# The last softmax-sum addition of a unit as an accumulating DMA, in a Macaron block on one Trainium2 core

## The chip, the cores and the metric

The kernel runs on one core of a Trainium2 chip. The metric is the device time of one execution in microseconds (us), as the median of several runs. The engines are named as in the profile: PE is TensorE's matmul row and PEld its weight loads, DVE is VectorE, ACT is ScalarE, POOL is GpSimd, SP is SyncE. "L797" is line 797 of the kernel before the change.

## The reference

Four sequences of 1024 tokens with 128 features pass through three residual steps:

```
x = x + 0.5 * ffn(layernorm(x))
x = x + attention(layernorm(x))        # attention adds its own input too
x = x + 0.5 * ffn(layernorm(x))

ffn:        8 experts; weights from a sigmoid router
            out = sum over e of w[e] * (silu(x Wg[e]) * (x Wu[e])) Wd[e]
attention:  h = layernorm(x) * scale + bias
            c_q, c_kv = h w_down_q^T, h w_down_kv^T          # 64 wide each
            q, k, v   = up-projections of them, 16 heads of 64; rotary on q and k
            out       = softmax(q k^T / 8) v, heads joined, times w_out^T, plus input
```

Everything is float32. The part that matters here is the softmax: each query's 1024 exponentials have to be summed, and that sum (the denominator) divides the query's output.

## The kernel before

The kernel has three stages that overlap at their edges: the first feed-forward (to about 220 us), attention (about 220 to 1490 us), and the second feed-forward.

Attention is cut into 64 **units** U. A unit is one pair of heads of one sequence and one half (512) of its queries. A unit has eight **slots**, one for each block of 128 keys; slot `s = 8 * U + c`. For a slot and each of the two heads `hh`, `score` (L781) makes a 128 x 512 block of transposed scores on PE, in four matmuls, the last of which subtracts the row maximum, and ACT (L785) writes its exponential to a tile `p` of 128 keys x 2 heads x 512 queries. There are eight `p` buffers, so a slot takes the buffer of the slot eight before it. `values` (L804) multiplies each `p` block with the latent values on PE and adds up the eight slots of a unit in the bank `psc`. `passA` (L755, L756) makes scores of units that come 15 slots later, from which DVE takes the row maxima; the maxima of a unit go through DRAM (`d<-m`, then `maxr<-d`) to become a row.

The **denominators** are made in two steps. First the eight `p` blocks of a unit are added element by element into a tile `acc` of 128 x 1024 float32. `accumulate` (L797) does that on POOL: the first addition joins slots 0 and 1, and each later slot adds one more, seven in all. Then `den` (L816) sums `acc` over its 128 keys: matmuls with a matrix of ones, four for the two heads' halves, into a PSUM tile that ACT copies to `dsb` (L818). From there the sums go through DRAM (L822, L824) to a column layout `dT`, and `outp` (L839 to L854) divides by them.

`direct(U)` says how many of a unit's last `p` blocks are left out of POOL's additions and go to `den` by themselves, as four more matmuls each on PE. Before the change it is 1 for every third unit up to U = 53 (18 units), and 0 for the others.

The order on every engine is written out by hand. The main loop runs over **groups** g of four slots, two groups to a unit. In a group the program issues, in this order: the score matmuls of four slots with the `passA` matmuls between them; after every second group `den` of the unit that ended one group earlier (`self.den(g // 2 - 1)`); some steps of the rotary embedding and some loads; then the values of the four slots before. So the scores of unit U are in groups 2U and 2U + 1, and `den(U)` stands on PE behind the scores of group 2U + 2 and ahead of the values of the second half of unit U.

POOL's queue holds, besides the additions, one subtraction of 128 x 1024 per step of the rotary embedding (L680, `eo<-eo,hi_r`, one per unit as long as that work lasts), and small pieces of the router and the norms. All DMAs are issued from SP's queue: heads' loads (`QT<-qs`, `KT<-ks`), loads for the rotary embedding (`C_l<-cs`) and its stores (`qs<-eo`, `qs<-hi_r` and the same for `ks`), and the small transfers of maxima and denominators. SP's queue is in order, and it waits for `d<-m` to land before it issues `maxr<-d`.

In the last unit, `den(63)` stands on PE ahead of the last values and of the second feed-forward.

Of the kernel before, what the change touches and what calls it, by code (L numbers as in the profile page):

```python
# [13 lines left out]
ALU = mybir.AluOpType  # L14
# [4 lines left out]
B, S, D = 4, 1024, 128  # L19
# [21 lines left out]

def direct(U):

    return 1 if U % 3 == 2 and U < 56 else 0


class Kernel:
# [741 lines left out]
    def accumulate(self, s):  # L789

        nc = self.nc
        U, c = divmod(s, 8)
        if c == 0:
            self.acc_of[U] = self.accp.tile([128, 2, 512], F32, name="acc")
        elif c < 8 - direct(U):
            acc = self.acc_of[U]
            nc.gpsimd.tensor_tensor(acc, self.p_of[s - 1] if c == 1 else acc, self.p_of[s], ALU.add)  # L797
# [10 lines left out]
    def den(self, U):  # L808

        nc = self.nc  # L810
        osb = self.osb_of[U] = self.op2.tile([128, 512], F32, name="osb")
        pd = self.aux()
        parts = [self.p_of[8 * U + c] for c in range(8 - direct(U), 8)] + [self.acc_of[U]]
        for k, part in enumerate(parts):
            for n in range(4):
                nc.tensor.matmul(pd[32 * n:32 * n + 32, 0:256], self.ones, part[:, n // 2, 256 * (n % 2):256 * (n % 2) + 256], start=k == 0, stop=k == direct(U))  # L816
        dsb = self.op1.tile([128, 256], F32, name="dsb")
        nc.scalar.copy(dsb, pd[:, 0:256])  # L818
        dT = self.ms.tile([128, 8], F32, name="dT")

        d1 = self.dram.tile([4, 256], F32, name=f"d1_{U % 4}")
        nc.sync.dma_start(out=d1, in_=dsb[0:128:32, :])  # L822
        last = U == 2 * 8 * B - 1
        self.at(self.group + 1, lambda: nc.sync.dma_start(out=dT, in_=d1.rearrange("(h x) (y p) -> p (h x y)", x=2, p=128)), "mid")  # L824
        self.at(self.group + (4 if last else 3), lambda: self.outp(U, osb, dT), "side")
# [328 lines left out]
```

## Time and profile before

| what | value |
|---|---|
| median of 3 runs | 1651.11 us (1650.53 to 1651.83) |
| profiled execution, own time from first to last instruction (span) | 1648.4 us |
| PE busy | 1593.2 us, 97% |
| PEld busy | 1033.2 us, 63% |
| DVE busy | 1317.6 us, 80% |
| ACT busy | 1013.5 us, 61% |
| POOL busy | 1456.0 us, 88% |
| DMA, SP's queue | 210.28 MB, 50.6% of 16 engines |
| POOL additions L797 | 430 of 2.38 us |
| den's matmul instructions L816 | 512 from `acc`, 144 from `p` |
| granted PE clock, mean | 0.994 |

The profile is of one execution. Its span goes from the first to the last instruction; the profile has no other time of its own for that execution, so the median of the runs is compared with the span. A group line reads: line, engine, operation, output <- inputs, shapes, count, then busy us and mean ns of one, then the idle time of that engine just before these instructions and what ended it. A wait line reads: who waited <- for whom: us in total, times, longest. A timeline line reads: start us, duration us, engine, line, operation, count, and in brackets the idle time before it. A float32 matmul appears as two instructions, so four matmuls of `den` are eight rows; their ends are modelled, so rows of PE overlap and the distance between starts is the better measure. Instructions that issue a DMA are not counted as busy.

### The profile page before, as it was taken

What the parts mean: (1) busy time and instruction counts of PE and PEld (TensorE: products, weight loads), DVE (VectorE), ACT (ScalarE), POOL (GpSimd) and SP (SyncE); (2) the same over time, 40 slices, a digit from 0 to 9 for tenths busy, and PEclk for the clock granted to TensorE, in tenths of its full rate; (3) what the DMA queues carried; (4) which work ended last, traced back from release to release, by engine and by line L of the source; (5) the groups of instructions that cost most, each with busy time, mean ns of one, the idle gap of its engine ahead of it and who ended that gap; (6) DMA issues with size and microseconds to landing.
All of it is one profiled execution on the core that took longest, in us unless ns stands there. A gap on an engine that the chain in (4) does not pass through costs nothing.

```text
span 1648.4 us, 31237 instructions
## 1 busy us (share of the span) xinstructions
PE 1593.2 (97%) x11044; PEld 1033.2 (63%) x11044; DVE 1317.6 (80%) x2417; ACT 1013.5 (61%) x2220; POOL 1456.0 (88%) x833
## 2 busy tenths in 40 slices
PE   7998989999999999999999999999999999998998
PEld 5876765566566665666565666666566655656776
DVE  6556668888988888888899889889988868616897
ACT  4675666666666666666666656666566655654555
POOL 5668889999999989999999999999999999895676
PEclk9999999999999999999999999999999999999999
DMA  7025557555555655555555556666655532114443
GB/s 226 1 65 166 155 141 168 142 142 130 134 140 140 142 142 134 146 140 138 131 138 142 129 143 152 150 147 141 141 140 149 130 66 53 36 57 138 140 133 103
DMA packets 241149, 212.28 MB, mean 129 GB/s; under 512 B 157664, under 2 KB 170592, under 8 KB 240224
## 3 DMA queue, kind: packets, MB, share of 16 engines
q1 hardware_dynamic: 240992, 210.28, 50.6%
q8 instruction: 87, 1.43, 0.4%
q14 instruction: 70, 0.57, 0.1%
HBM read 130.39 MB, written 79.82 MB: 128 GB/s over the span
## 4 chain that ended last, share of the span: by engine, by line
PE 68%; POOL 3%; DVE 3%; ACT 2%; issue 2%; POOLq 0%; DVEq 0%; ACTq 0%
PE psc L804 24%; PE ps_s L781 21%; PE ps_a L755 6%; PE psx L781 3%; PE ps_s L521 3%; PE ps_s L816 2%; PE psx L476 2%; PE psx L839 2%; POOL acc L797 2%; PE psx L647 2%; ACT p L785 1%; PE ps_s L839 1%; POOL p L529 1%; PE psc L521 1%; DVE m L756 1%
## 5 line engine op out<-in xcount | busy, mean ns | idle before, releaser
L797 POOL TENSOR_TENSOR acc<-acc,p 128x1024 f32<-128x1024 f32 x366 | 872.6, 2384 | 56.3 <-ACT p L785 30.8
L756 DVE TENSOR_REDUCE m<-ps_a 128x1 f32<-128x512 f32 x1024 | 684.8, 688 | 158.0 <-PE ps_a L755 136.2
L785 ACT ACTIVATE p<-ps_s 128x512 f32<-128x512 f32 x896 | 478.2, 602 | 230.7 <-PE ps_s L781 197.1
L781 PE MATMUL ps_s<-QT,KT 64*128 64x512 f32 x2688 | 548.3, 397 | 3.1 <-DVE eo L663 3.0
L804 PE MATMUL psc<-p,ckn 128*64 128x512 f32 x2048 | 468.8, 600 | 0.0
L781 PEld LDWEIGHTS ps_s<-QT,KT 64*128 64x128 f32 x2688 | 351.2, 185 | 138.8 <-issue 76.3
L755 PE MATMUL ps_a<-KT,QT 64*128 64x512 f32 x1024 | 417.9, 419 | 5.0 <-DVE m L756 3.5
L804 PEld LDWEIGHTS psc<-p,ckn 128*64 128x64 f32 x2048 | 135.8, 137 | 257.3 <-issue 252.3
L781 PE MATMUL ps_s<-maxr,one_row 64*128 64x512 f32 x896 | 237.0, 391 | 0.0
L755 PEld LDWEIGHTS ps_a<-KT,QT 64*128 64x128 f32 x1024 | 184.5, 184 | 36.4 <-DVE m L756 12.8
L797 POOL TENSOR_TENSOR acc<-p 128x1024 f32<-128x1024 f32 x64 | 152.4, 2381 | 14.2 <-ACT p L785 11.9
L806 ACT COPY osb<-psc 128x512 f32<-128x512 f32 x64 | 37.6, 587 | 193.3 <-PE psc L804 193.3
L680 POOL TENSOR_TENSOR eo<-eo,hi_r 128x1024 fp32r<-128x1024 f32 x55 | 132.0, 2400 | 0.0
L781 PEld LDWEIGHTS ps_s<-maxr,one_row 64*128 64x128 f32 x896 | 122.3, 185 | 13.5
L781 PE MATMUL psx<-QT,KT 64*128 64x512 f32 x384 | 110.2, 393 | 0.0
L529 POOL TENSOR_TENSOR p<-eo,p 128x512 fp32r<-128x512 f32 x42 | 62.7, 1499 | 40.6 <-ACT p L528 33.1
L425 POOL TENSOR_TENSOR X<-X,dtmp 128x512 f32<-128x512 f32 x54 | 69.1, 1280 | 32.1 <-ACT dtmp L424 31.0
L852 DVE SCALAR_TENSOR_TENSOR X<-ps_s,rT,X 128x128 f32<-128x128 f32 x248 | 68.8, 339 | 26.4 <-PE ps_s L839 26.4
L849 ACT ACTIVATE psx<-psx,rT 128x128 f32<-128x128 f32 x248 | 85.4, 344 | 6.0
L672 ACT CAST hi_r<-eo 128x512 fp32r<-128x512 f32 x128 | 72.9, 615 | 18.8 <-POOL eo L667 14.0
L785 ACT ACTIVATE p<-psx 128x512 f32<-128x512 f32 x128 | 76.9, 601 | 4.4 <-issue 2.1
L781 PEld LDWEIGHTS psx<-QT,KT 64*128 64x128 f32 x384 | 71.1, 185 | 8.5
(237 smaller groups left out, 2388.2 us busy)
## 6 DMA issues: line engine op xcount, KB each, us to landing
C_l<-cs SPq DMA_DIRECT2D x128, 256.0 KB
QT<-qs SPq DMA_DIRECT2D x256, 128.0 KB
KT<-ks SPq DMA_DIRECT2D x256, 128.0 KB
qs<-hi_r SPq DMA_DIRECT2D x32, 512.0 KB
qs<-eo SPq DMA_DIRECT2D x32, 512.0 KB
ks<-hi_r SPq DMA_DIRECT2D x32, 512.0 KB
ks<-eo SPq DMA_DIRECT2D x32, 512.0 KB
rt<-wt SPq DMA_DIRECT2D x52, 256.0 KB
```

Source lines behind the costliest of these rows:

```text
L425: nc.gpsimd.tensor_tensor(X[:, t:t + 4, :], X[:, t:t + 4, :], tmp, ALU.add)
L529: (nc.gpsimd if m < N - 1 else nc.vector).tensor_tensor(sh[:, 1, :], hp, self.f(sh[:, 0, :]), ALU.subtract)
L672: nc.scalar.copy(w["hi"][:, k, :], w["eo"][:, k, :])
L680: nc.gpsimd.tensor_tensor(w["eo"].bitcast(F32R), w["eo"], self.f(w["hi"]), ALU.subtract)
L755: nc.tensor.matmul(self.psA[hh], self.QT[P % 3][r, 0, q0:q0 + 128], self.KT[P % 3][r, 0, kk * 512:kk * 512 + 512], start=True, stop=True)
L756: nc.vector.tensor_reduce(m[0][:, hh, qb, kk:kk + 1], self.psA[hh], AX.X, ALU.max)
L781: nc.tensor.matmul(ps, w, x, start=k == 0, stop=k == 3)
L785: nc.scalar.activation(self.p_of[s][:, hh, :], ps, AF.Exp, scale=0.125)
L797: nc.gpsimd.tensor_tensor(acc, self.p_of[s - 1] if c == 1 else acc, self.p_of[s], ALU.add)
L804: nc.tensor.matmul(self.psC[64 * hh:64 * hh + 64, :], self.ckn[b % 2][:, c, :], self.p_of[s][:, hh, :], start=c == 0, stop=c == 7)
L849: nc.scalar.activation(po[0][:, c], po[0][:, c], AF.Identity, scale=rT[:, i:i + 1])
L852: nc.vector.scalar_tensor_tensor(x, po[1][:, i * 128:(i + 1) * 128], rT[:, 4 + i:5 + i], x, ALU.mult, ALU.add)
```

## The change

The seventh addition (slot 7) of every unit but the last is no longer an instruction of POOL's but a DMA, issued from POOL's queue, which adds the tile `p` of slot 7 to `acc` in place. `direct` is 0 for those units, so no `p` block goes to PE by itself. For the last unit (U = 63) `direct` is 3: POOL makes four additions (slots 0 to 4), and the blocks of slots 5, 6 and 7 go to `den` as twelve more matmuls. The last line of the diff only makes the end of `den`'s accumulation follow the number of blocks.

```diff
 def direct(U):
 
-    return 1 if U % 3 == 2 and U < 56 else 0
+    return 3 if U == 2 * 8 * B - 1 else 0
...
         if c == 0:
             self.acc_of[U] = self.accp.tile([128, 2, 512], F32, name="acc")
+        elif c == 7 and not direct(U):
+            nc.gpsimd.dma_start(out=self.acc_of[U], in_=self.p_of[s], accum_op=ALU.add)
         elif c < 8 - direct(U):
             acc = self.acc_of[U]
             nc.gpsimd.tensor_tensor(acc, self.p_of[s - 1] if c == 1 else acc, self.p_of[s], ALU.add)
...
         for k, part in enumerate(parts):
             for n in range(4):
-                nc.tensor.matmul(pd[32 * n:32 * n + 32, 0:256], self.ones, part[:, n // 2, 256 * (n % 2):256 * (n % 2) + 256], start=k == 0, stop=k == direct(U))
+                nc.tensor.matmul(pd[32 * n:32 * n + 32, 0:256], self.ones, part[:, n // 2, 256 * (n % 2):256 * (n % 2) + 256], start=k == 0, stop=k == len(parts) - 1)
```

The DMA reads `p` and `acc` and writes `acc`. It waits for the sixth addition and for the exponentials of slot 7; `den` waits for it, and so do the next user of that `p` buffer (slot 7 of the next unit) and of that `acc` buffer (two units later).

## The prediction

> **What bounds the kernel now.** The page's busy shares come first, then the costliest groups, then the waits. TensorE is busy for 97% of the span and GpSimd for 88%; the windows of 100 us from 250 to 1350 us show TensorE at 98 to 100 and GpSimd at 93 to 97.
>
> ```profile
> PE 1593.2 (97%) x11044; PEld 1033.2 (63%) x11044; DVE 1317.6 (80%) x2417; ACT 1013.5 (61%) x2220; POOL 1456.0 (88%) x833
> L797 POOL TENSOR_TENSOR acc<-acc,p 128x1024 f32<-128x1024 f32 x366 | 872.6, 2384 | 56.3 <-ACT p L785 30.8
> L797 POOL TENSOR_TENSOR acc<-p 128x1024 f32<-128x1024 f32 x64 | 152.4, 2381 | 14.2 <-ACT p L785 11.9
> ```
>
> GpSimd's 430 additions are 1025 us of its 1456. But being busy is not being waited for. The waits, longest first, have only these rows in which TensorE waits for an addition (the first is its weight load, which runs ahead):
>
> ```profile
> PEld ps_s L816 <- POOL acc L797: 6.8, 1, 6.8
> PE ps_s L816 <- POOL acc L797: 5.9, 1, 5.9
> ```
>
> One wait in 64 units, and the timeline places it in the last unit. GpSimd is nearly full, yet in the other 63 units it finishes in time. So what it is relieved of is worth little; what TensorE is relieved of, or made to wait for, counts. TensorE runs its program in order: a wait of den's matmuls holds up the values and scores queued behind them.
>
> **What is taken off.** GpSimd: 18 direct units have 6 additions and 46 have 7, 430 in all; afterwards 63 have 6 and the last has 4, 382 in all. 48 x 2.38 us = 114 us of GpSimd, off the path by the reading above: I count it at nothing. What hides it is TensorE's own work in each unit; ACT's waits on L797, 10.5 us in four places, are the most that it could return, and only the range has them.
>
> TensorE: den's group for a direct unit is this, in the timeline.
>
> ```profile
> 704.98 0.64 PE L816 MATMUL ps_s<-p,ones 128*32 128x256 f32 x8
> 705.44 0.61 PE L816 MATMUL ps_s<-acc,ones 128*32 128x256 f32 x8
> 705.99 3.65 PE L804 MATMUL psc<-p,ckn 128*64 128x512 f32 x16
> ```
>
> The p part delays the acc part by 0.46 us. From den to den, units 15 to 53 take 19.98 us after a direct den and 19.65 after another: of 0.45 us of TensorE, 0.33 reaches the time, a factor of 0.73 (the rest was VectorE's and ScalarE's to wait for anyway). 18 x 0.33 = 6.0 us gained; 8.1 if all counted.
>
> The last unit:
>
> ```profile
> 1477.64 3.65 PE L804 MATMUL psc<-p,ckn 128*64 128x512 f32 x16
> 1487.18 1.08 PE L816 MATMUL ps_s<-acc,ones 128*32 128x256 f32 x8 [5.89 <-POOL acc L797]
> ```
>
> Its additions on GpSimd start at 1468.85 and 1471.29 (two), then, after two L173 pieces, at 1477.49 (four to 1487.12). With four in all the last ends near 1479.9, before TensorE is free at 1481.29. So 5.9 us go, and three more blocks cost 3 x 0.45 = 1.3: 4.6 gained, and the feed-forward behind it starts that much earlier. Gains together: 6.0 + 4.6 = 10.6 us.
>
> **What is added.** 63 accumulating DMAs of 512 KB, each behind the sixth addition on GpSimd's queue, and den waits for their landing. Behind the DMA's issue stand L680's subtraction and the next unit's first addition, which had 2.4 us of the seventh addition in its place; an issue under 2.4 us delays nobody (SP's take 0.3 to 0.6). Behind den's wait on TensorE stand 16 values matmuls and the next group. The allowance can be read, here in unit 45:
>
> ```profile
> 1129.47 10.10 POOL L797 TENSOR_TENSOR acc<-acc,p 128x1024 f32<-128x1024 f32 x4 [0.74 <-ACT p L785]
> 1142.12 0.64 PE L816 MATMUL ps_s<-acc,ones 128*32 128x256 f32 x8
> ```
>
> These are additions 4 to 7. The sixth ends after three, at 1136.8, and den starts at 1142.1: 5.3 us. A lighter GpSimd does not bring that forward: the fourth addition had waited for ScalarE's exponentials (0.74), so the sixth ends three additions after those. The same reading in all 63 units has a median of 4.9 us, with 8 in 10 between 3.8 and 5.8.
>
> No row has an accumulating transfer, nor any on GpSimd's queue. The nearest are SP's:
>
> ```profile
> 1125.78 0.39 SPq L56 DMA_DIRECT2D qs<-eo  x1
> 1138.75 0.34 SPq L56 DMA_DIRECT2D d<-m  x1
> 1140.85 0.57 SPq L56 DMA_DIRECT2D maxr<-d  x1
> ```
>
> maxr<-d waits for d<-m, so 4 KB have landed 2.1 us after issue; on average it is 0.34 of issue and 158.1 / 64 = 2.47 of wait, 2.8. For the 512 KB of qs<-eo, the DMA view of 1126 to 1129 us shows its first bytes at 1126.7 and some 380 GB/s: one pass takes 1.4 us. An addition must read both operands, so I take two passes: 2.1 + 2.8 = 4.9 us in quiet, 2.8 + 2.8 = 5.6 on average. The DMA engines are 42 to 62% busy in four such allowances; I take 5.2. Bounds: one pass and a quiet fixed part, 3.5; at worst SP's longest wait and its issue, 4.8, with two passes at the 269 GB/s of 1137.3 to 1139.0, 3.9: 8.7.
>
> The excess over the allowance, unit by unit and summed over the 63: 4.6 us at a latency of 3.5, 13.6 at 4.5, 34.2 at 5.2, 115 at 6.6, 247 at 8.7. With the factor 0.73: 3.4, 9.9, 25.0, 84 and 180. At 5.2 the balance is 25.0 - 10.6 = +14.4 us; break-even is a latency of 4.55.
>
> The Trainium skill's page "DMA: Bandwidth & Descriptors", in "Anatomy of one DMA", gives a transfer of GpSimd's queue 2.0 us and bytes over 436 GB/s: as an estimate 3.2 us here, which would hide it and leave about -8 us. "Collectives: The Full Stack", under "The bandwidth ceiling", speaks against the change: an add in the DMA engines needs two source reads and halves the rate; both pages together give an estimate of 4.4 us, a balance of -2. No run here shows either; the sum above uses neither.
>
> The other load: the transfers add 63 x 2.8 = 176 us at full rate to a DMA share of 51% of the span, some 11 points. SP's loads of the next pair and of C_l are issued a group (9.7 us) or more ahead, so I cost the collisions at nothing beyond the latency; without that cover, one C_l late by 0.5 us in each of the 55 steps that L680 counts would cost 0.73 x 27 = 20 us.
>
> The profiled execution's span is 1648.4 us, 2.7 below the runs' median of 1651.11. 1648.4 + 14.4 = 1662.8, and with that offset 1665.5.
>
> **Rivals.** *The transfer is hidden* (latency under 4.3 us). For it: den comes a whole score phase after the exponentials, and one pass is only 1.4 us. Then 3 to 9 us of excess remain against 10.6: 1643 to 1648. With no excess, all 8.1 us of the direct blocks and 7 us of ACT's waits, 1648.4 - 8.1 - 4.6 - 7 + 2.7 = 1631. This ends on the faster side and decides from 4.3 us down. *The add is slow in the DMA engines* (8.7 us or more): every unit waits, 180 us: about 1821. Against it: the DMA share has room, and TensorE's clock and SP's rate show no strain. *GpSimd's issue costs as much as the addition that it replaces:* then GpSimd keeps 18 x 2.4 us more than before, with L680 and the next additions late by that; GpSimd's idle time before additions, 70 us in all, takes it, and the time stays near that of the forecast. *The change does nothing but move the tail*, if the queue's transfer lands exactly at den: 1651 - 4.6 = 1646.5, within the first rival.
>
> **How the numbers follow.** The measurement can tell 0.2%, 3.3 us. Waits of 0.2 to 2 us a unit (latency 4.7 to 7): 0.45, and this is the forecast. Slow add (above 7 us): 0.11. Hidden: 0.38. Balanced within 3.3 us (4.3 to 4.7): 0.06. So faster 0.38, same 0.06, slower 0.56. The forecast's own range is 1654 to 1743, the ends of that latency by the same sum. The range of 8 in 10 takes in most of the hidden case, from 1638 (no excess and 8.1 us of direct blocks), and ends at a latency of 6.6 us: 1648.4 + 84 - 10.6 + 2.7 = 1724.
>
> **What would show it.** Right: den's L816 is preceded on TensorE by idle time put down to a DMA, in most units, 0.5 us on average; 382 additions; GpSimd's share falls to near 82%; the last unit's 5.9 us gone. Wrong: no idle time at L816 and a spacing near 19.6 us (hidden), or 3 us and more in every unit (slow add). A GpSimd issue above 2.4 us, or SP's loads found late by TensorE, would break the two terms that I cost at nothing.

## The result and the profile after

The changed kernel runs at 1788.5 us (median of 4 runs, 1779.3 to 1791.5) against 1650.8 for the kernel before on the same chip: 1.0817 times as long, interval 1.0797 to 1.0838. The direction of the forecast came true; the size was 137.7 us where 14.4 were forecast. The profiled execution's span is 1787.1 us, 138.7 more than before, and the mean granted TensorE clock is 0.971 where it was 0.994.

The code has moved by two lines: the DMA is L796, the additions are L799, the values L806, den L818. From the page: busy shares, GpSimd's DMA queue, the chain that ended last by engine, three groups, and the DMA issues.

```profile
PE 1628.2 (91%) x10924; PEld 1041.5 (58%) x10924; DVE 1323.4 (74%) x2417; ACT 1014.5 (57%) x2220; POOL 1398.6 (78%) x848
...
q0 software_dynamic: 9072, 33.03, 9.5%
...
PE 32%; DMA 20%; POOL 16%; issue 7%; ACT 5%; DVE 1%; SPq 1%; POOLq 0%; DVEq 0%; ACTq 0%
...
L799 POOL TENSOR_TENSOR acc<-acc,p 128x1024 f32<-128x1024 f32 x318 | 754.2, 2372 | 220.7 <-ACT p L785 201.0
...
L806 PE MATMUL psc<-p,ckn 128*64 128x512 f32 x2048 | 502.6, 636 | 0.0
...
L818 PE MATMUL ps_s<-acc,ones 128*32 128x256 f32 x512 | 44.1, 415 | 108.5 <-DMA acc<-p 107.0
...
acc<-p POOLq DMA_DIRECT2D x63, 512.0 KB, 6.7
```

From the page of before, the chain and the values:

```profile
PE 68%; POOL 3%; DVE 3%; ACT 2%; issue 2%; POOLq 0%; DVEq 0%; ACTq 0%
...
L804 PE MATMUL psc<-p,ckn 128*64 128x512 f32 x2048 | 468.8, 600 | 0.0
```

GpSimd is relieved as computed (318 + 64 = 382 additions). Its busy time falls by 57.4 us only, not by 114: the 63 issues, 0.88 us each, are counted in it here, unlike SP's, and L680's subtractions have become slower. Before its additions it now stands idle for 220.7 us in place of 56.3, 201.0 of them for ScalarE's exponentials, where it was 30.8. Den waits 107.0 us for the DMA, where before it waited 5.9 us for an addition, once. The chain is the largest contrast: before it was 68% TensorE and 3% GpSimd; now it is 32% TensorE, 20% this DMA and 16% GpSimd. One transfer takes 6.7 us from issue to landing (4.5 to 9.1), where the prediction took 5.2 from the end of the sixth addition.

The values (L806) have the same number of instructions as before and 502.6 us of busy time where it was 468.8, 33.8 more. TensorE's rows of the timeline show where that comes from: two units in a row, the first of which did not have to wait.

```profile
1212.37 0.64 PE L818 MATMUL ps_s<-acc,ones 128*32 128x256 f32 x8
1212.94 3.65 PE L806 MATMUL psc<-p,ckn 128*64 128x512 f32 x16
1222.25 3.65 PE L806 MATMUL psc<-p,ckn 128*64 128x512 f32 x16
1234.54 0.64 PE L818 MATMUL ps_s<-acc,ones 128*32 128x256 f32 x8 [3.11 <-DMA acc<-p]
1235.11 5.35 PE L806 MATMUL psc<-p,ckn 128*64 128x512 f32 x16
```

After a stand of 3.11 us the same 16 instructions take 5.35 us in place of 3.65. The windows (span of the window, then busy us and counts of PE, PEld, DVE, ACT, POOL, then granted clock, DMA share, GB/s) say why:

```profile
1225.00:1231.00 6.00, 6.00 (x50) 4.34 (x48) 4.92 (x9) 3.56 (x7) 5.62 (x6) 1.00 1.02 215
1235.00:1238.30 3.30, 3.30 (x14) 1.03 (x12) 1.18 (x3) 0.37 (x1) 3.22 (x2) 0.58 0.06 0
```

The granted clock falls from 1.00 to 0.58 just behind the stand. So the two large entries are 107.0 - 5.9 = 101.1 us of waiting and 33.8 us of slower values, 134.9 of the 138.7.

Why the waits add up, and are not absorbed, stands in the chain of the same unit, from den to den, in order of time (start, length, what):

```profile
1212.44 0.57 PE ps_s L818 x8
1213.01 3.58 PE psc L806 x16
1216.60 1.12 PE ps_s L781 x5
...
1218.06 1.10 ACT p L785 x2
...
1219.22 0.95 POOL acc L799
1220.17 1.48 issue
...
1221.69 2.36 POOL acc L799
...
1224.13 2.38 POOL acc L799
...
1226.81 7.59 DMA acc<-p
1234.40 0.14 issue
1234.54 0.59 PE ps_s L818 x5
```

It is a closed loop. Den holds up the values behind it, these hold up the next scores, the scores hold up the exponentials, those the fourth addition, then follow the fifth, the sixth and the DMA, and the DMA holds up the next den. One turn is 1234.54 - 1212.44 = 22.1 us, and that has become the unit: from den to den, units 2 to 54 take 22.2 us on average (19.9 to 24.7) where they took 19.8 (19.0 to 21.0). As an estimate from these pieces: with an addition of 2.4 us where the transfer and its handovers take 8.0, the turn would be 16.5 us, and TensorE's own work would set the time, as it did before.

### The profile page after: what moved, and what is told of

Same layout as the page of the kernel before. It is cut to its first block, busy times and chain, and to the rows that moved or that the text cites. A ratio compares the mean times of both kernels' runs of the same rounds, so it can differ in the third digit from the quotient of the medians.

```text
span 1787.1 us, 31134 instructions
## 1 busy us (share of the span) xinstructions
PE 1628.2 (91%) x10924; PEld 1041.5 (58%) x10924; DVE 1323.4 (74%) x2417; ACT 1014.5 (57%) x2220; POOL 1398.6 (78%) x848
## 4 chain that ended last, share of the span: by engine, by line
PE 32%; DMA 20%; POOL 16%; issue 7%; ACT 5%; DVE 1%; SPq 1%; POOLq 0%; DVEq 0%; ACTq 0%
DMA acc<-p 20%; POOL acc L799 15%; PE psc L806 15%; PE ps_s L781 6%; ACT p L785 3%; PE ps_s L521 3%; PE ps_s L818 2%; PE psx L476 2%; PE ps_a L755 1%; PE psc L521 1%; POOL p L529 1%; SPq L56 1%; PE psx L781 0%; PE psx L841 0%; ACT psx L851 0%
## 5 line engine op out<-in xcount | busy, mean ns | idle before, releaser
L799 POOL TENSOR_TENSOR acc<-acc,p 128x1024 f32<-128x1024 f32 x318 | 754.2, 2372 | 220.7 <-ACT p L785 201.0
L781 PE MATMUL ps_s<-QT,KT 64*128 64x512 f32 x2688 | 547.2, 398 | 3.4 <-DVE eo L663 2.7
L806 PE MATMUL psc<-p,ckn 128*64 128x512 f32 x2048 | 502.6, 636 | 0.0
L781 PEld LDWEIGHTS ps_s<-QT,KT 64*128 64x128 f32 x2688 | 351.5, 185 | 139.1 <-issue 79.5
L806 PEld LDWEIGHTS psc<-p,ckn 128*64 128x64 f32 x2048 | 143.9, 145 | 285.9 <-issue 280.6
L781 PE MATMUL ps_s<-maxr,one_row 64*128 64x512 f32 x896 | 236.9, 392 | 0.0
L799 POOL TENSOR_TENSOR acc<-p 128x1024 f32<-128x1024 f32 x64 | 161.3, 2520 | 19.2 <-ACT p L785 19.2
L680 POOL TENSOR_TENSOR eo<-eo,hi_r 128x1024 fp32r<-128x1024 f32 x55 | 147.9, 2689 | 0.0
L818 PE MATMUL ps_s<-acc,ones 128*32 128x256 f32 x512 | 44.1, 415 | 108.5 <-DMA acc<-p 107.0
L781 PEld LDWEIGHTS ps_s<-maxr,one_row 64*128 64x128 f32 x896 | 122.4, 185 | 14.2
L781 PE MATMUL psx<-QT,KT 64*128 64x512 f32 x384 | 110.2, 392 | 0.0
L820 ACT COPY dsb<-ps_s 128x256 f32<-128x256 f32 x64 | 23.8, 371 | 129.9 <-PE ps_s L818 123.8
L425 POOL TENSOR_TENSOR X<-X,dtmp 128x512 f32<-128x512 f32 x54 | 69.2, 1281 | 34.8 <-ACT dtmp L424 33.8
L818 PEld LDWEIGHTS ps_s<-acc,ones 128*32 128x32 f32 x512 | 12.2, 110 | 133.1 <-issue 96.2
```

Source lines behind the costliest of these rows:

```text
L425: nc.gpsimd.tensor_tensor(X[:, t:t + 4, :], X[:, t:t + 4, :], tmp, ALU.add)
L680: nc.gpsimd.tensor_tensor(w["eo"].bitcast(F32R), w["eo"], self.f(w["hi"]), ALU.subtract)
L781: nc.tensor.matmul(ps, w, x, start=k == 0, stop=k == 3)
L806: nc.tensor.matmul(self.psC[64 * hh:64 * hh + 64, :], self.ckn[b % 2][:, c, :], self.p_of[s][:, hh, :], start=c == 0, stop=c == 7)
```

## The experiments

Each run was timed beside the kernel before; the ratios are to that. All kernels start from the changed one, except where it is said.

| kernel | us | ratio, interval |
|---|---|---|
| changed | 1788.5 | 1.0817 [1.0797, 1.0838] |
| last unit alone | 1645.0 | 0.9946 [0.9932, 0.9960] |
| seven additions, no transfer | 1656.6 | 1.0032 [1.0020, 1.0044] |
| late additions, no transfer | 1828.7 | 1.1070 [1.1054, 1.1087] |
| TensorE kept busy | 1761.4 | 1.0650 [1.0631, 1.0669] |
| plain copy | 1718.6 | one run |
| half the transfer | 1693.4 | 1.0248 [1.0220, 1.0277] |
| transfer into a spent tile | 1690.4 | 1.0235 [1.0218, 1.0252] |
| den behind the values | 1689.1 | 1.0219 [1.0181, 1.0256] |
| den one group later | 1688.5 | 1.0212 [1.0193, 1.0231] |
| the same, no transfer | 1661.5 | 1.0046 [1.0031, 1.0061] |
| the same, C_l earlier | 1662.9 | 1.0079 [1.0057, 1.0101] |
| the same, half the transfer | 1661.1 | 1.0057 [1.0035, 1.0079] |

**The last unit alone.** The kernel before, with only the last unit's part of the change.

```diff
-    return 1 if U % 3 == 2 and U < 56 else 0
+    return 3 if U == 2 * 8 * B - 1 else 1 if U % 3 == 2 and U < 56 else 0
```

> The kernel before with one thing of the change: the last unit sends three blocks to TensorE and GpSimd makes four additions there. The prediction's term is 4.6 us of gain: 1646 to 1648 us. Rival: the feed-forward behind it waits for something else at its start (the weights' pieces on GpSimd, the loads), and the time is within 1.5 us of before.

1645.0 us. By the ratio, against the kernel before on the same chip, the gain is 8.9 us (6.6 to 11.2), more than the term of 4.6 us. The profiled spans, 1643.9 and 1648.4, differ by 4.5, but they are of single executions on two chips. The gain is there, and it is at least of the forecast's order. This kernel is faster than both.

**Seven additions everywhere, no transfer.** The rest of the change without the DMA: GpSimd makes the seventh addition itself in 63 units.

```diff
-        elif c == 7 and not direct(U):
-            nc.gpsimd.dma_start(out=self.acc_of[U], in_=self.p_of[s], accum_op=ALU.add)
```

> The changed kernel without the transfer: GpSimd makes all seven additions in every unit but the last, no block goes to TensorE, and the last unit has its three blocks on TensorE. It has 445 additions, 63 more than the changed kernel and 15 more than before. By the prediction's terms, GpSimd's relief is worth nothing and the gains of 6.0 and 4.6 us stay: 1636 to 1645 us. Rival: GpSimd, at 93 to 97 per cent, has no room for the 18 additions that the blocks on TensorE had taken from it; then den waits for additions in those units and the time is 1651 us or more.

1656.6 us, 11.6 more than with the 18 direct blocks in place (14 by the two ratios, as the runs were on two chips). GpSimd is at 90% (1491.1 us), and den now waits for it:

```profile
PEld ps_s L816 <- POOL acc L797: 27.9, 30, 2.7
...
PE ps_s L816 <- POOL acc L797: 15.4, 17, 2.2
```

The weight load runs ahead of the matmul, so these rows overlap and are not summed. Nearly all of the 138 us belongs to the transfer: without it the same kernel is 132 us faster. But GpSimd was at its edge: 18 additions more were not free.

**Late additions, no transfer.** Is it DMA at all, or only lateness? Here GpSimd's own last additions are made as late as the transfer's landing.

```diff
-        elif c == 7 and not direct(U):
-            nc.gpsimd.dma_start(out=self.acc_of[U], in_=self.p_of[s], accum_op=ALU.add)
...
-            nc.gpsimd.tensor_tensor(acc, self.p_of[s - 1] if c == 1 else acc, self.p_of[s], ALU.add)
+            if direct(U) or c not in (2, 3):
+                nc.gpsimd.tensor_tensor(acc, self.p_of[s - 1] if c == 1 else acc, self.p_of[s], ALU.add)
+            for _ in range(2 if c == 7 else 0):
+                nc.gpsimd.tensor_tensor(acc, acc, self.p_of[s], ALU.add)
```

> No transfer at all: GpSimd leaves slots 2 and 3 out of the sums and adds slot 7 twice more, so that it makes as many additions as with seven, but the last one ends some 7.3 us after the sixth used to, about where the transfer landed. Theory A: den stands as long as in the changed kernel, the granted clock falls to about 0.97 and the time is 1765 to 1800 us. If the clock and a part of the time were the transfers' doing: clock 0.99 and 1700 to 1745 us (63 units by 2.1 us by the factor 0.73, less the gains).

1828.7 us. The page of this kernel has the same two marks, den's wait and slow values:

```profile
L807 PE MATMUL psc<-p,ckn 128*64 128x512 f32 x2048 | 520.4, 655 | 0.0
...
L819 PE MATMUL ps_s<-acc,ones 128*32 128x256 f32 x512 | 42.2, 402 | 135.9 <-POOL acc L800 135.9
```

So neither the stand nor the slower clock needs a DMA; a late `acc` is enough.

**TensorE kept busy.** Twelve matmuls of den's form, whose results nobody uses, stand ahead of den in the 63 units.

```diff
+        for _ in range(3 if not direct(U) else 0):
+            for n in range(4):
+                nc.tensor.matmul(pd[32 * n:32 * n + 32, 0:256], self.ones, self.p_of[8 * U + 6][:, n // 2, 256 * (n % 2):256 * (n % 2) + 256], start=True, stop=True)
```

> The changed kernel with twelve matmuls of the same form as den's put ahead of den in the 63 units with a transfer, on a block that is there already and into the bank that den then overwrites; they are 1.35 us of work that fills a part of TensorE's stand. Theory A2 (about 105 us of standing and, beside it, 34 us of matmuls at the halved clock that is granted after a stand of some 2 us or more): the stand falls by what the matmuls fill, the landing is not later, most halvings go, the granted clock returns to 0.98 to 0.99 and the time is 1755 to 1772 us although TensorE does 85 us more work. Rival (the clock falls with the load of the DMA engines, not with the stand): the clock stays at 0.97 and the time at 1785 to 1795 us, more where the added work is not hidden.

1761.4 us, by the two ratios some 27 less although TensorE has more work. The mean clock is 0.992 and the values are back at 471.1 us:

```profile
L806 PE MATMUL psc<-p,ckn 128*64 128x512 f32 x2048 | 471.1, 602 | 0.0
```

The landing is not earlier (6.9 us), so what this undoes is the clock's part, and the clock is worth some 27 us; the loop is still there, and den still waits.

**Plain copy.** How much of the landing time is the addition itself?

```diff
-            nc.gpsimd.dma_start(out=self.acc_of[U], in_=self.p_of[s], accum_op=ALU.add)
+            nc.gpsimd.dma_start(out=self.acc_of[U], in_=self.table[:, 1, :].rearrange("p (h q) -> p h q", h=2))
```

> The changed kernel, where the transfer from GpSimd's queue is a plain copy of 512 KB of another tile over acc in place of an accumulation, so that the sums are not those of the softmax; den waits for it as before. If the accumulation costs a second pass (a packet of 4 KB at 0.33 us in place of half that), the eight packets of an engine take 1.4 us when nothing else runs in place of 2.75, issue to landing falls from 6.7 to about 5.0 us, and the time to 1700 to 1750 us. If it is the fixed part (the issue, the first packet 2.3 us after it) that makes den late, the landing stays above 6 us and the time above 1770.

1718.6 us. From the page, GpSimd's queue, the issue's median and den:

```profile
q0 software_dynamic: 9072, 33.03, 5.7%
...
L818 PE MATMUL ps_s<-acc,ones 128*32 128x256 f32 x512 | 42.0, 397 | 64.7 <-DMA acc<-table 59.9
...
acc<-table POOLq DMA_DIRECT2D x63, 512.0 KB, 5.8
```

Per transfer and DMA engine that is 0.057 x 1716.6 / 63 = 1.55 us, against 0.095 x 1787.1 / 63 = 2.69 us for the accumulation; a 4 KB packet takes 0.161 us and 0.328 us in the two traces. The accumulation costs the time of a second pass. But landing falls only from 6.7 to 5.8 us, not to 5.0: the time of a packet is halved, and 87% of the landing time stays.

**Half the transfer.** The DMA takes head 0's half (256 KB), GpSimd adds the other half after issuing it.

```diff
-            nc.gpsimd.dma_start(out=self.acc_of[U], in_=self.p_of[s], accum_op=ALU.add)
+            acc = self.acc_of[U]
+            nc.gpsimd.dma_start(out=acc[:, 0, :], in_=self.p_of[s][:, 0, :], accum_op=ALU.add)
+            nc.gpsimd.tensor_tensor(acc[:, 1, :], acc[:, 1, :], self.p_of[s][:, 1, :], ALU.add)
```

> The changed kernel, where the accumulating transfer carries head 0's half alone (256 KB) and GpSimd adds the other half itself after issuing it. Latency as read from the changed trace: 0.3 of handover, 2.3 to the first packet, half of 3.7 for the packets, 0.4 to the semaphore, so 4.9 us in place of 6.7 to 7.0, right at den's allowance of 4.9 us: the wait at den falls from 107 to some 30 us and the time to 1685 to 1720. By the prediction's own terms (5.2 us, of which 2.8 goes by the bytes) the wait would be gone, 1650 to 1665. If the latency hardly goes by the bytes: above 1770.

1693.4 us; the landing's median is 4.8 us, and the values' group, den's group and den's wait for the DMA are

```profile
L808 PE MATMUL psc<-p,ckn 128*64 128x512 f32 x2048 | 471.1, 602 | 0.0
...
L820 PE MATMUL ps_s<-acc,ones 128*32 128x256 f32 x512 | 40.9, 388 | 45.2 <-DMA acc<-p 35.4
...
PE ps_s L820 <- DMA acc<-p: 35.4, 31, 3.0
```

With 0.3 us of handover the latency is 5.1 us. That makes this nearly the kernel which the prediction had in mind: at 5.2 us its sum of the excess over the allowances is 34.2 us, and den waited 35.4 for the DMA and 45.2 in all. The table of excesses was near. Its price was not: the forecast at that latency was 1665, and 1693 came, at a mean clock of 0.991 and with values hardly slower than before.

**Transfer into a spent tile.** The DMA adds to the tile of the unit before, so that den has nothing to wait for.

```diff
-            nc.gpsimd.dma_start(out=self.acc_of[U], in_=self.p_of[s], accum_op=ALU.add)
+            nc.gpsimd.dma_start(out=self.acc_of[U - 1 if U else U], in_=self.p_of[s], accum_op=ALU.add)
```

> The changed kernel with the transfer adding to the tile of the unit before, which den has read already; slot 7 is left out of the sums of 62 units. The same transfers are issued at the same places, but no den waits for them. Theory A (the wait at den and the clock after it): 1636 to 1650 us. Theory B (traffic, issue, SP's later landings): above 1740 us; anything between is the share that the traffic has.

1690.4 us, with a landing of 5.2 us in the median, but it does not separate what it was meant to. The tile is the one that the next unit's first addition writes, so that addition now waits for the landing, and den waits for the additions:

```profile
POOL acc L799 <- DMA acc<-p: 127.0, 56, 5.3
...
PE ps_s L818 <- POOL acc L799: 30.7, 24, 3.0
```

The wait was moved, not removed.

**Den behind the values.** Den's matmuls are issued after the group's four values in place of ahead of them, some 4 us later.

```diff
-                self.den(g // 2 - 1)
...
+            if g and g % 2 == 0:
+                self.den(g // 2 - 1)
```

(The second place is behind the loop over the group's values.)

> The changed kernel with den's matmuls moved behind the values of the four slots that follow it, so that the landing has 3.65 us of TensorE work more. Theory A: the changed kernel is slow because TensorE stands at den until the transfer has landed (7.0 us after the sixth addition against an allowance of some 5), and because the clock granted to it is halved after such a stand. Then the allowance is some 8.5 us, few units wait, the clock is back near 0.99 and the time is 1638 to 1655 us. Theory B: the transfers themselves (traffic on the DMA engines, the issue on GpSimd's queue, SP's transfers that land later) stretch the units, and the wait at den is only where it shows. Then the idle time moves to another line and the time stays above 1740 us.

1689.1 us. Den's wait is down to 4.3 us, and a new one stands in its place: the next scores (L781) need the bank that den has just written and ScalarE has not yet copied.

```profile
PEld ps_s L781 <- ACT dsb L819: 57.1, 63, 1.0
...
PE ps_s L781 <- ACT dsb L819: 28.0, 57, 0.5
```

**Den one group later.** To have neither wait, den is issued a group (10 us) later; the step that uses its sums keeps its place.

```diff
-        self.at(self.group + (4 if last else 3), lambda: self.outp(U, osb, dT), "side")
+        self.at(self.group + (4 if last else 2), lambda: self.outp(U, osb, dT), "side")
...
-                self.den(g // 2 - 1)
+                self.osb_den[g // 2 - 1] = self.osb_of[g // 2 - 1] = self.op2.tile([128, 512], F32, name="osb")
+            if g == NGRP or (g > 2 and g % 2):
+                self.den(NGRP // 2 - 1 if g == NGRP else (g - 3) // 2)
```

> The changed kernel with den one group (9.7 us) later on TensorE, at the same place within the group, outp where it was; the last unit as in the changed kernel. The landing then has some 14 us, and the bank that den uses is not one that the scores behind it need at once. Theory A (wait and clock): no wait at den, the clock above 0.99, and the time is 1636 to 1645 us, below the kernel before. Theory B (the transfers' traffic and GpSimd's issue cost time by themselves, which the two earlier ways of removing the wait, both at 1689 to 1690 us, leave possible): 1670 to 1690 us again.

1688.5 us, 100 less than the changed kernel. No wait at den is left, though the transfer itself now lands after 7.3 us in the median; the main waits of TensorE on DMAs are these:

```profile
PEld ps_s L647 <- DMA C_l<-cs: 11.6, 9, 2.9
...
PE ps_s L647 <- DMA C_l<-cs: 7.7, 9, 2.5
...
PE psx L647 <- DMA C_l<-cs: 6.9, 4, 3.0
```

SP's loads for the rotary embedding arrive late. Three more kernels take this apart.

*The same without the transfer* (GpSimd makes the seventh addition):

> The kernel without the transfer (seven additions on GpSimd in 63 units, three blocks of the last unit on TensorE) with den one group later. If what made that kernel 5 us slower than before was den waiting for the seventh addition, the waits go and the time is 1638 to 1648 us. If GpSimd's amount of work is the bound of a unit (7 additions and one subtraction, 19.5 us, and the small pieces, in a unit of 19.7), moving den does not help: 1652 to 1660 us, and only the transfer, which takes 2.4 us of GpSimd's work away, would make the difference to the kernel with den a group later.

1661.5 us, and no row of C_l. The difference of 27 us lies where SP's loads run: from den to den, units 15 to 47 take 20.8 us on average with the transfer and 20.0 without; units 54 to 63, which have no rotary loads beside them, take 18.65 in the median in both. In those units GpSimd issues its transfers all the same, so the issue costs nothing that can be seen.

*The same, with C_l fetched one group earlier*, and the transfer in place:

```diff
-        ROPE = {"mid": {2: "dhi"}, "side": {0: "mm"}, "end": {-1: "fetch", 0: "vector", 2: "dlo"}, "cast": {1: "hi0 hi1 lo"}}
+        ROPE = {"mid": {2: "dhi"}, "side": {0: "mm"}, "end": {-2: "fetch", 0: "vector", 2: "dlo"}, "cast": {1: "hi0 hi1 lo"}}
```

> The kernel with den one group later, with the fetch of C_l also one group (about 10 us) earlier, so that a transfer late by some microseconds is still in time. Theory (the accumulating transfers make SP's loads late, and TensorE's stands for C_l bring halved clock with them): the waits on C_l of 26 us in that kernel go, and with them some half of its 42 us of halved clock, so 1645 to 1665 us in place of 1688.5. Rival (what is lost there is GpSimd's: its issue of the transfer and its slower other work): C_l earlier changes nothing, 1685 to 1690. Rival (SP's queue as a whole is late, dT and the maxima too): C_l's waits go but turn up at dT or at the maxima, 1670 to 1685.

1662.9 us: C_l's waits are gone, and the ratio falls from 1.0212 to 1.0079, where the kernel without a transfer has 1.0046. So some four fifths of what the transfer costs there are C_l's lateness.

*The same, with half the transfer:*

> The kernel with den one group later, where the accumulating transfer carries head 0's half alone (256 KB) and GpSimd adds the other half itself. It ran at 1688.5 us with the whole transfer and at 1661.5 with none. Theory (the loss beside SP's loads goes by the bytes that the transfer moves): about half of the 27 us is left, 1668 to 1678. Rival (the loss comes with each issue, whatever its size): 1686 to 1692.

1661.1 us, no more than with none, and 0.3 us as TensorE's only matmul wait for C_l. The loss does not go by the bytes in proportion, as was expected; half the transfer stays under the margin that C_l has. Since each unit still has one issue, the rival that charges the issue is out.

## Why the prediction was right or wrong

**What held.** *382 additions, GpSimd near 82%* (78% of a longer span). *An issue under 2.4 us delays nobody:* it takes 0.88 us, and the kernels with den later show no price for it; the rival of a dear issue falls. *The last unit's gain of 4.6 us* came, and by the ratio it was larger, 8.9 us (6.6 to 11.2). *Two passes, 2.8 us:* 2.69 per transfer, and the plain copy takes 1.55. *The excess over the allowances* was near: 34.2 us summed for a latency of 5.2, and 35.4 measured, 45.2 with den's other waits, where the half transfer takes 5.1. *"GpSimd's relief at nothing":* the three later-den kernels run at 1661 to 1663 us with GpSimd between 1403 and 1492 us busy. The opposite direction is not free: 18 additions more cost 12 to 14 us net, so the direct blocks did work that the profile of before did not show as a wait.

**The rivals.** Nothing is hidden, so the faster side is out. The slow add was priced at 8.7 us of latency and 1821 us; the transfer has 7.0 and the result lies between that and the forecast's own upper end of 1743, at what the prediction gave a chance of 0.11 (above 7 us) or just below it.

**What failed, first: the latency of 5.2 us.** It is 7.0 from the end of the sixth addition to the landing: 0.3 of handover, which the sum did not have, and 6.7 by the DMA row. In the trace the first packet moves 2.3 us after the start of the issue, the packets then take 3.7 us in the median (2.75 when nothing else runs, up to 5.3 beside other traffic), and some 0.3 follow. The prediction's fixed part of 2.1 to 2.8 was SP's for a whole 4 KB transfer; here 2.3 are gone before the first byte. And its 2.8 for the bytes was the quiet value, while the transfer meets SP's loads and stores: in the unit shown above, 512 KB of `qs<-hi_r` were issued 0.75 us behind it, and the DMA engines are full in the window from 1225 us (a share of 1.02). By the prediction's own table a latency of 6.6 is 115 us of excess, and 7.0, between that and 247 at 8.7, some 140; den's row has 107.0, 1.7 us a unit where 0.5 was written down. At the prediction's own price of 0.73 these 72.8 us more of waiting are 53 of the 123 us between 1665.5 and 1788.5. Nor is the latency a constant: the same 512 KB landed after 5.2 us in the median with the spent tile and after 7.3 with den a group later.

**Second: the factor 0.73.** It was read from what a direct block's 0.45 us of TensorE cost in a unit that TensorE set. A wait at den is another thing: it lies in the loop shown above and comes back at the next den in full. Taking the last unit's 4.6 us as the only gain, the time lost is 137.7 + 4.6 = 142.3 us in the changed kernel, and den's whole idle time, 108.5, with the 33.8 us of slower values makes just that. With half the transfer it is 42.4 + 4.6 = 47.0 against 45.2 + 2.3; with the plain copy 67.6 + 4.6 = 72.2 against 64.7 + 9.2; with the late additions 177.0 + 4.6 = 181.6 against 135.9 + 51.6. So a microsecond of standing at den costs a whole one, not 0.73, and the halved clock, for which the prediction had no term, comes on top; it is small with half the transfer and large where the stands are long. Price and clock together are another 64 us of the miss (142.3 - 0.73 x 107.0); the remaining 6 are the direct blocks' gain, which this account leaves out. (The last unit's gain is itself uncertain by some 4 us.) The prediction had even noted that the fourth addition waits for ScalarE's exponentials, which is one link of that loop, and did not follow it on: those wait for scores, these stand behind values, and the values behind den.

**Third: collisions with SP's loads at nothing.** In the changed kernel itself this holds: TensorE's matmuls wait for C_l once, 0.2 us, presumably because den's waits leave the loads time. But as soon as den's wait is taken away it costs 27 us, near the 20 us that the prediction gave for C_l late by 0.5 us in 55 steps. SP's queue itself is held up too: its wait for `d<-m` (64 times) rose from 158.1 to 306.5 us, and in the unit shown SP issued `d<-m` at 1228.18 and could issue `maxr<-d` only at 1235.51, after the accumulation had landed at 1234.40:

```profile
1228.18 0.34 SPq L56 DMA_DIRECT2D d<-m  x1
1235.51 0.56 SPq L56 DMA_DIRECT2D maxr<-d  x1
```

Everything behind it on SP's queue moves with it; C_l is on that queue. The wait for `d<-m` is longer in the later-den kernels as well, with the transfer (243.8) and without it (203.7), so it is not the transfer's alone.

**The pages.** "DMA: Bandwidth & Descriptors" ("Anatomy of one DMA") of the Trainium skill gave an estimate of 3.2 us; 6.7 were measured, with 4.5 as the least of 63. Together with the halved rate of "Collectives: The Full Stack" it was 4.4. The halved rate agrees with the packets (0.328 against 0.161 us); the latency does not.

**What stays open.** The 6.0 us of the direct blocks were not measured by themselves: every kernel here that lacks them has longer waits at den, a fuller GpSimd or a moved den. The later-den kernels have the same floor of 1661 us whatever the transfer, 16 above the best one; what that placement costs was not followed.

## What to carry to other kernels

Before a wait is priced, follow what stands behind it on its engine until the chain either ends in slack or comes back to the wait. If it comes back, add up one turn: as long as it is shorter than the unit, the wait is free, and above that every microsecond counts in full, and more if TensorE's clock falls. A transfer's latency in a loaded kernel is not its quiet one: take the start, the bytes at the rate that is left beside the traffic, and the handovers on both sides.

## What the runs showed of the hardware that was not expected

- The granted clock falls to half for 3.4 us (twice for 6.8) behind short stands of TensorE. Between 300 and 1600 us of the changed kernel, 21 such stretches follow its 54 stands of over 0.7 us: no stand under 1.8 us lost the clock by itself, between 1.8 and 2.8 us it went either way, and above that each lost it. The trace shows what decides in between: all 26 slow stretches of the kernel start on one grid of 3.413 us. Cut by that grid, each of the 21 starts behind a cell in which TensorE was idle for 1.72 us or more; in the 357 cells that were followed by one at full clock it was idle for at most 1.74. With the late additions the same split lies at 1.8 us. So here a cell that was idle for about half its length cost the clock, and a stand that falls on two cells could be longer. "TensorE: Matmul & The Clock Gate" of the Trainium skill ("Part 1: The HAM clock gate") puts the idle window at about 3.4 us. The length of the slow stretches agrees with that figure; the stands that set them off were mostly shorter.
- A transfer from GpSimd's queue has its first packet 2.3 us after the start of its issue (median; 1.4 to 4.7). With the spent tile it is 1.5 in the median.
- GpSimd's own work beside the accumulation is slower: L680, the subtraction that follows the issue, takes 2.69 us in place of 2.40, and 2.67 with half the transfer. With the plain copy it takes 2.42.
